# Graph attention on one core: part of the weighted row sums moved to TensorE, h.u as a matmul, q kept in SBUF, and the short last tile transferred in two pieces

## The chip, the core and the metric

The kernel runs on one core of a Trainium2 chip. The core has five engines with queues of their own: TensorE (PE, matrix products; loading of the stationary operand is shown as PEld), VectorE (DVE), ScalarE (ACT), GpSimd (POOL) and SyncE (SP). SP, ACT and POOL issue DMA transfers. SBUF is the on-chip working memory with 128 partitions; PSUM is the accumulator memory that TensorE writes. The metric is the time of one execution in device microseconds (us), lower is better. The kernel before is timed in three runs; a profile comes from one more execution.

## The reference: what is computed

One layer of graph attention over N = 3327 nodes with D = 1024 features, in float32. With h the layer-normed x passed through a ReLU:

```python
f = h @ Wf + bf
g = h @ Wg + bg
e = relu(f @ g.T)
scores = where(adj > 0, e, -9e15)
out = x + softmax(scores, axis=1) @ (h @ W + bW)
```

The adjacency matrix has few ones: a node has at most some 37 neighbours. So for node i only its neighbours j are needed:

- score(i, j) = relu(h_j . q_i + c_i), where q_i = A^T h_i + v with A = Wf Wg^T, v = Wg bf, and c_i = h_i . u + c with u = Wf bg, c = bf . bg;
- y_i = the sum over the neighbours of softmax weight times h_j;
- out_i = x_i + y_i W + bW.

## The kernel before

The program has two stages on the core.

**The first stage** walks over 26 tiles of 128 nodes; the last holds 127, since 3327 = 25 x 128 + 127. For each tile, `degrees` (L428) loads the rows of adj into `a` (L431, on SP's queue), turns them to float with their row sum on ACT (L433) and multiplies by the column number on POOL (L434). `normed` (L400) loads the x rows into `xt` (L404, SP), normalizes them and writes them to the DRAM table `hd` (L426, ACT's queue). `edges` (L439) picks the neighbour lists with MAX8 on DVE (L443 to L454); `store_lists` (L468) writes them to the DRAM table `pd`. Beside that `make_A` (L502) builds the product A on TensorE and ScalarE, 128 rows at a time, and u, which L517 makes as a row repeated in all partitions (`u_sb`). At the end the nodes are sorted by their number of neighbours; L583 writes the permutation `perm`. After it `make_rows` (L520) makes the constants; the last of its copies, on DVE, is L354.

**The second stage** walks over 26 tiles of the sorted nodes. `CAPS` gives the largest number of neighbours in each tile, from 37 down to 11. For a tile s:

- `prepare(s)` (L635) gathers the lists (`pi`) and the rows of h (`hp`) with indirect DMA on POOL, transposes hp on TensorE (`hT`), multiplies by A into `q` in PSUM (L648, L649), and takes c_i = h.u + c on DVE with a multiply-and-sum over 1024 elements (L658, into `ci`).
- `dot(s, k)` (L665) gathers the rows of the k-th neighbour of all 128 nodes into one of 23 buffers `G` (L669, POOL) and multiplies them with q on DVE, adding ci (L671). Each such instruction is followed by a short one that reads the accumulator.
- `softmax` (L676) turns the scores into weights `sc`: maximum on DVE, exp on ACT (L687). A tile with more than 20 neighbours is done in two chunks, and the second rescales y by `al` (L692).
- `combine` (L700) makes y, the weighted sum: the first neighbour on ACT (L709), every further one as one multiply-add on DVE (L711), in a chain over y. For two chunks y is divided by the sum of weights on ACT (L713).
- `project(s)` (L715) gathers the x rows (`xp`), transposes y on TensorE (L619) with copies to SBUF on ACT (L620), and multiplies by W (L726, L727). `finish(s)` (L730) adds x on DVE (L735) and scatters the rows to the output (L736, POOL).

TensorE does a float32 product as two instructions, so eight products show as 16.

The order of the program is the loop at the end: prepare one tile ahead, the dots of a chunk, finish of the tile before, softmax, the first three dots of the next chunk, combine, project. The framework plans from this the order of each engine's instructions, by its own estimate of times, and places the waits; an instruction that is ready can be put ahead of an earlier one that is not. On the chip each engine keeps to the planned order. Buffers are limited: 23 for G, two for hp, y and xp, one for hT; a gather waits until the buffer's last reader is done.

## Time and profile before

| What | Value |
|---|---|
| median of three runs | 1794.35 us (1793.04 to 1795.7) |
| profiled execution, its own time | 1794.12 us |
| its span, first to last instruction | 1792.4 us |
| mean granted TensorE clock | 0.81 |
| busy: DVE, PE, POOL, ACT | 82%, 60%, 46%, 17% of the span |
| q0 (POOL's indirect transfers) | 286.92 MB |
| all transfers | 372.37 MB, mean 208 GB/s |

A line of a group names the source line, the engine, the operation, what it writes and reads, the shapes and the count; then busy us and mean ns of one, and the idle time of the engine just before such instructions with what ended most of it. A line of the timeline names start and length in us, engine, line and operation; in square brackets stand the idle time before it and what released it. A DMA line names the queue's engine, the count, KB each and the median us from issue to landing. Times in windows count from the start of the span.

### The profile page before, as it was taken

How to read it: one execution, taken by the hardware profiler on the slowest of the kernel's cores; microseconds unless marked ns; L12 is line 12 of the kernel's file. 1: busy time of each engine (PE TensorE's matmuls, PEld its weight loads, DVE VectorE, ACT ScalarE, POOL GpSimd, SP SyncE). 2: the span in 40 equal slices, each digit the busy share in tenths (PEclk: the TensorE clock that was granted, in tenths of full speed). 3: DMA queues.
4: the chain of work that ended last, by engine and by line, in shares of the span. 5: the costliest groups of instructions: out<-in, count | busy, mean ns of one | idle time of the engine just before them, and what ended most of it. 6: DMA issues, size and time to landing. Idle time of an engine off the chain costs nothing.

```text
span 1792.4 us, 10947 instructions
## 1 busy us (share of the span) xinstructions
PE 1069.6 (60%) x2824; PEld 493.0 (28%) x2824; DVE 1478.6 (82%) x2798; ACT 296.9 (17%) x480; POOL 827.9 (46%) x625
## 2 busy tenths in 40 slices
PE   1278980354007736477364777766686959697833
PEld 1134440021003313133131333323332424233311
DVE  5877860377999899999999999999999899988850
ACT  6666650100001011011000000000000001000100
POOL 7667570115455344553455544444454445435510
PEclk9999995567558868788687888888898979898866
DMA  8888850029678576773676655655665656646320
GB/s 319 306 329 298 292 190 27 28 84 376 210 233 292 168 223 222 236 238 137 222 270 224 242 214 191 226 197 211 212 244 203 232 191 252 205 170 214 100 65 17
DMA packets 124312, 372.37 MB, mean 208 GB/s; under 512 B 40905, under 2 KB 41305, under 8 KB 120913
## 3 DMA queue, kind: packets, MB, share of 16 engines
q0 software_dynamic: 106288, 286.92, 46.8%
q1 hardware_dynamic: 10800, 70.49, 10.7%
q10 hardware_dynamic: 7152, 14.18, 2.1%
q8 instruction: 24, 0.39, 0.1%
q14 instruction: 48, 0.39, 0.1%
HBM read 343.63 MB, written 27.80 MB: 207 GB/s over the span
## 4 chain that ended last, share of the span: by engine, by line
DVE 27%; PE 27%; issue 22%; POOL 9%; DMA 7%; another core or an unknown queue 4%; ACT 2%; POOLq 0%; ACTq 0%; DVEq 0%
DVE y L711 15%; PE ps_o L726 14%; PE q L648 8%; POOL r L434 5%; DVE junk L671 5%; DMA G<-hd,pi 4%; POOL G L608 3%; DVE cand L443 2%; PE ps_A L511 2%; PE ps_t L619 2%; DMA hd<-xt 1%; ACT r L433 1%; DVE sc L671 1%; DVE lst L450 1%
## 5 line engine op out<-in xcount | busy, mean ns | idle before, releaser
L608 POOL DMA_INDIRECT G<-hd,pi x468 | 505.2, 1080 | 418.8 <-DVE y L711 163.3
L671 DVE CUSTOM_DVE_ANT_0 junk<-G,q,ci 128x1024 bf16<-128x1024 f32 (+1 forms) x468 | 597.3, 1276 | 44.6 <-DMA G<-hd,pi 26.4
L711 DVE SCALAR_TENSOR_TENSOR y<-G,sc,y 128x1024 f32<-128x1024 f32 (+1 forms) x442 | 566.2, 1283 | 32.1 <-ACT y L709 23.0
L726 PE MATMUL ps_o<-W_sb,yT 128*128 128x512 f32 (+1 forms) x832 | 402.6, 640 | 1.3 <-ACT yT L620 1.3
L648 PE MATMUL q<-A_sb,hT 128*128 128x512 f32 (+1 forms) x832 | 372.6, 601 | 14.1 <-ACT hT L620 7.5
L619 PE MATMUL ps_t<-ident,y 128*128 128x128 f32 (+1 forms) x208 | 48.1, 408 | 488.6 <-DVE y L711 267.9
L434 POOL TENSOR_TENSOR r<-r,iotaj 128x3327 f32<-128x3327 f32 (+1 forms) x26 | 188.3, 7250 | 131.8 <-ACT r L433 127.4
L726 PEld LDWEIGHTS ps_o<-W_sb,yT 128*128 128x128 f32 (+1 forms) x832 | 166.9, 207 | 207.0 <-issue 198.1
L648 PEld LDWEIGHTS q<-A_sb,hT 128*128 128x128 f32 (+1 forms) x832 | 154.4, 190 | 201.6 <-issue 187.4
L619 PEld LDWEIGHTS ps_t<-ident,y 128*128 128x128 f32 (+1 forms) x208 | 38.7, 214 | 495.6 <-issue 273.1
L443 DVE MAX8 cand<-r 128x8 f32<-128x208 f32 (+2 forms) x416 | 134.0, 360 | 47.9 <-POOL r L434 47.9
L511 PE MATMUL ps_A<-WgT,WfT 128*128 128x512 f32 x256 | 126.3, 655 | 0.5 <-ACT WfT L483 0.5
L620 ACT COPY yT<-ps_t 128x512 f32<-128x512 f32 (+1 forms) x52 | 29.9, 585 | 521.3 <-PE ps_t L619 521.3
L608 POOL DMA_INDIRECT hp<-hd,perm x26 | 27.8, 1068 | 172.0 <-PE ps_t L619 118.7
L433 ACT ACTIVATE r<-a 128x3327 f32<-128x3327 int32 (+1 forms) x26 | 77.1, 2967 | 56.4 <-DMA a<-in_adj_dram 54.7
L608 POOL DMA_INDIRECT xp<-in_x_dram,perm x26 | 34.6, 1329 | 94.7 <-DMA out_dram<-xp,perm 83.1
L410 DVE BATCH_NORM_STATS2 st<-xt 128x6 f32<-128x512 f32 (+1 forms) x26 | 17.7, 680 | 69.2 <-DMA xt<-in_x_dram 69.2
L511 PEld LDWEIGHTS ps_A<-WgT,WfT 128*128 128x128 f32 x256 | 53.0, 211 | 76.6 <-issue 68.4
L687 ACT ACTIVATE sc<-sc,nm 128x11 f32<-128x11 f32 (+11 forms) x32 | 9.8, 308 | 372.6 <-DVE nm L683 272.6
L620 ACT COPY hT<-ps_t 128x512 f32<-128x512 f32 (+1 forms) x52 | 28.0, 588 | 251.4 <-PE ps_t L619 226.8
L736 POOL DMA_INDIRECT out_dram<-xp,perm x26 | 31.8, 1222 | 74.0 <-DVE rs L696 34.0
L466 PE MATMUL pre<-oh,low 128*128 128x64 bf16 x26 | 5.4, 207 | 101.5 <-DVE hit L463 101.5
(131 smaller groups left out, 746.9 us busy)
## 6 DMA issues: line engine op xcount, KB each, us to landing
a<-in_adj_dram SPq DMA_DIRECT2D x25, 1663.5 KB, 9.4
xt<-in_x_dram SPq DMA_DIRECT2D x25, 512.0 KB, 4.3
hd<-xt ACTq DMA_DIRECT2D x25, 512.0 KB, 6.7
G<-hd,pi POOLq DMA_INDIRECT x468, 5.9
wr<-in_L_gnn_Wg_dram SPq DMA_DIRECT2D x8, 512.0 KB, 6.4
wr<-in_L_gnn_Wf_dram SPq DMA_DIRECT2D x8, 512.0 KB, 6.6
W_sb<-in_L_gnn_W_dram SPq DMA_DIRECT2D x1, 4096.0 KB
a<-in_adj_dram SPq DMA_DIRECT2D x1, 1650.5 KB
```

Of the source, the lines that this page charges most:

```text
L433: nc.scalar.activation(r[:n], a[:n], AF.Relu, accum_out=deg[:n, t : t + 1])
L434: nc.gpsimd.tensor_mul(r[:n], r[:n], iotaj[:n])
L443: nc.vector.max(cand[:n, s * 8 : s * 8 + 8], r[:n, s * SW : min(N, (s + 1) * SW)])
L511: nc.tensor.matmul(ps, WfT[:, k, :], WgT[:, k, o * CB : (o + 1) * CB], start=(k == 0), stop=(k == KD - 1))
L608: nc.gpsimd.indirect_dma_start(out=to, out_offset=None, in_=table, in_offset=bass.IndirectOffsetOnAxis(ap=idx, axis=0),)
L619: nc.tensor.transpose(ps[:, k, :n], of[:n, (g + k) * P : (g + k + 1) * P], ident[:n, :n])
L620: nc.scalar.copy(to[:, g : g + 4, :n], ps[:, :, :n])
L648: nc.tensor.matmul(qo, hT[:, k, :n], A_sb[:, k, o * CB : (o + 1) * CB], start=(k == 0), stop=False)
L671: nc.vector.tensor_tensor_reduce(junk[:n], g[:n], e["q"][:n], 1.0, e["ci"][:n], op0=ALU.mult, op1=ALU.add, accum_out=e["sc"][:n, k : k + 1],)
L711: nc.vector.scalar_tensor_tensor(y, G[s, k][:n], p, y, op0=ALU.mult, op1=ALU.add)
L726: nc.tensor.matmul(ps[:n], yT[:, k, :n], W_sb[:, k, o * CB : (o + 1) * CB], start=(k == 0), stop=False)
L736: ins = nc.gpsimd.indirect_dma_start(out=out[:, :], out_offset=bass.IndirectOffsetOnAxis(ap=perm[:n, s : s + 1], axis=0), in_=e["xp"][:n], ...
```

## The change

Three things are changed.

1. **The short tile's transfers.** A new `pieces(t)` cuts the 127 rows of the last tile into 112 and 15. The loads of x and adj, the store of hd and the store of the lists issue one transfer for each piece. Tiles of 128 rows are one piece as before. The indirect transfers of the second stage are not cut.
2. **h.u and q.** u is made as a column per 128 features (`uT`), and `prepare` multiplies hT by it on TensorE: eight products with one column into a PSUM tile, from which ACT makes ci, adding c. L658 and its DVE instruction are gone. q goes to PSUM in halves, and ACT copies each half to a tile in SBUF (`qpool`, two buffers). The call of prepare moves from the start of tile s (for s + 1) to the end of tile s (for s + 2), after project(s); prepare(0) and prepare(1) stand before the loop. The PSUM room that q leaves takes the new tile `yT_ps`.
3. **A part of the weighted sums on TensorE.** `on_tensor` picks m neighbours of a tile's last chunk, m = (4 cap - 52) / 5 rounded down, at least 0 and at most two less than the chunk has, spread evenly and never k = 0. For each of them ACT makes a diagonal matrix from the weights (`diag`, four buffers), and TensorE multiplies the eight 128-column blocks of G by it, which adds the weighted rows, already transposed, in `yT_ps`. The other neighbours stay on DVE. In project, y is added to the same PSUM tile by eight products with the identity, in place of its eight transposes; where m is 0 the transposes stay. The division by the sum of weights is now made on the weights (sc) and on al, ahead of the rescaling of y, so L713 is gone.

```diff
+    def pieces(t):
+        n = rows(t)
+        m = n - n % 16
+        return [(0, m), (m, n - m)] if 0 < m < n else [(0, n)]
...
-            nc.sync.dma_start(xt[:n], x[t * P : t * P + n, :])
+            for a, m in pieces(t):
+                nc.sync.dma_start(xt[a : a + m], x[t * P + a : t * P + a + m, :])
...
-                nc.tensor.matmul(ps, bgr[:, k, :], WfT[:, k, :], start=(k == 0), stop=(k == KD - 1))
-            nc.scalar.copy(u_sb[:, c * P : (c + 1) * P], ps)
+                nc.tensor.matmul(ps[:, 0:1], WfT[:, k, :], bgT[:, k : k + 1], start=(k == 0), stop=(k == KD - 1))
+            nc.scalar.copy(uT[:, c : c + 1], ps[:, 0:1])
...
-        q = p_q.tile([P, D], FP, name="q")
+        q = e["q"] = qpool.tile([P, D], FP, name="q")
...
+            nc.scalar.copy(q[:n, o * CB : (o + 1) * CB], ps[:n])
+        ps = p_t.tile([P, 4, P], FP, name="ps_t")
+        for k in range(KD):
+            nc.tensor.matmul(ps[:n, 0, 0:1], hT[:, k, :n], uT[:, k : k + 1], start=(k == 0), stop=(k == KD - 1))
+        ci = e["ci"] = small.tile([P, 1], FP, name="ci")
+        nc.scalar.activation(ci[:n], ps[:n, 0, 0:1], AF.Identity, bias=c_sb[:n])
...
-        nc.vector.tensor_tensor_reduce(
-            junk[:n], hp[:n], u_sb[:n], 1.0, c_sb[:n], op0=ALU.mult, op1=ALU.add, accum_out=ci[:n]
-        )
...
+        if last:
+            rs = small.tile([P, 1], FP, name="rs")
+            nc.vector.reciprocal(rs[:n], l[:n])
+            if k0:
+                nc.vector.tensor_tensor(al[:n], al[:n], rs[:n], op=ALU.mult)
+            nc.vector.tensor_scalar(sc, sc, rs[:n], None, op0=ALU.mult)
+        if k0:
             nc.scalar.activation(e["y"][:n], e["y"][:n], AF.Copy, scale=al[:n])
...
+    def on_tensor(s, k0, k1):
+        m = min(max(0, (4 * CAPS[s] - 52) // 5), k1 - k0 - 2)
+        ks = range(max(k0, 1), k1)
+        return [k for i, k in enumerate(ks) if (i + 1) * m // len(ks) > i * m // len(ks)]
...
+            if k in pe:
+                diag = dpool.tile([P, P], FP, name="diag")
+                nc.scalar.activation(diag[:n, :n], ident[:n, :n], AF.Copy, scale=p)
+                if e["yT"] is None:
+                    e["yT"] = p_y.tile([P, KD, P], FP, name="yT_ps")
+                for c in range(KD):
+                    nc.tensor.matmul(
+                        e["yT"][:, c, :n], g[:n, c * P : (c + 1) * P], diag[:n, :n],
+                        start=(k == pe[0] and c % 4 == 0), stop=False, skip_group_check=True,
+                    )
...
+            for c in range(KD):
+                nc.tensor.matmul(
+                    e["yT"][:, c, :n], e["y"][:n, c * P : (c + 1) * P], ident[:n, :n],
+                    start=False, stop=(c % 4 == 3), skip_group_check=True,
+                )
+            for g in range(0, KD, 4):
+                nc.scalar.copy(yT[:, g : g + 4, :n], e["yT"][:, g : g + 4, :n])
...
     prepare(0)
+    prepare(1)
     for i, (s, k0, k1) in enumerate(units):
-        if not k0 and s + 1 < NT:
-            prepare(s + 1)
...
             project(s)
+            if s + 2 < NT:
+                prepare(s + 2)
```

More of the change, by code (lines that the diff above doesn't have):

```diff
@@ L333, in edge_path @@
     A_sb = wts.tile([P, KD, D], FP, name="A_sb")
-    u_sb = wts.tile([P, D], FP, name="u_sb")
+    uT = wts.tile([P, KD], FP, name="uT")
     c_sb = wts.tile([P, 1], FP, name="c_sb")
@@ L425, in normed @@
             nc.scalar.activation(xt[:n], xt[:n], AF.Relu, bias=nmr[:n], scale=rstd[:n])
-            nc.scalar.dma_start(hd[t * P : t * P + n, :], xt[:n])
+            for a, m in pieces(t):
+                nc.scalar.dma_start(hd[t * P + a : t * P + a + m, :], xt[a : a + m])
         def degrees(t):
@@ L430, in degrees @@
             a = apool.tile([P, N], I32, name="a")
-            nc.sync.dma_start(a[:n], adj[t * P : t * P + n, :])
+            for b, m in pieces(t):
+                nc.sync.dma_start(a[b : b + m], adj[t * P + b : t * P + b + m, :])
             r = kpool.tile([P, N], FP, name="r")
@@ L474, in store_lists @@
             if t1 > full:
-                nc.scalar.dma_start(pd[full * P :, :], pay[: rows(full), full, :])
+                for b, m in pieces(full):
+                    nc.scalar.dma_start(pd[full * P + b : full * P + b + m, :], pay[b : b + m, full, :])
         def transposed(to, of):
@@ L604, in edge_path @@
     p_t = ctx.enter_context(tc.tile_pool(name="p_t", bufs=2, space=PSUM))
+    p_y = ctx.enter_context(tc.tile_pool(name="p_y", bufs=1, space=PSUM))
     p_o = ctx.enter_context(tc.tile_pool(name="p_o", bufs=2, space=PSUM))
@@ L620, in transposed2 @@
             nc.scalar.copy(to[:, g : g + 4, :n], ps[:, :, :n])
-    def times(pool, name, lT, w_sb, b3, n):
-        halves = []
-        for o in range(OH):
-            ps = pool.tile([P, CB], FP, name=f"{name}{o if pool is p_q else ''}")
-            for k in range(KD):
-                nc.tensor.matmul(ps[:n], lT[:, k, :n], w_sb[:, k, o * CB : (o + 1) * CB], start=(k == 0), stop=False)
-            nc.tensor.matmul(ps[:n], ones3[:, :n], b3[:, o * CB : (o + 1) * CB], start=False, stop=True)
-            halves.append(ps)
-        return halves
     st = {}
@@ L776, in edge_path @@
     nc.vector.tensor_reduce(bad, bads, AX.X, ALU.max)
-    onesf = small.tile([P, P], FP, name="onesf")
+    onesf = small.tile([P, 1], FP, name="onesf")
     nc.vector.memset(onesf, 1.0)
```

31 lines of the change are left out of this document (14 added, 17 removed).

## The prediction

> **What bounds the kernel now.** I read the busy table by stages first, then the groups of the second half, then the timeline where the table shows a hole. Columns of the stage table: PE, PEld, DVE, ACT, POOL busy us with instruction counts, granted TensorE clock, DMA share, GB/s.
>
> ```profile
> 269.00:339.00 70.00, 0.22 (x1) 0.10 (x1) 0.78 (x2) 5.01 (x7) 8.85 (x2) 0.52 0.06 26
> 590.00:905.00 315.00, 186.87 (x466) 83.57 (x465) 298.47 (x423) 32.69 (x60) 144.42 (x135) 0.79 0.65 210
> 1250.00:1600.00 350.00, 270.41 (x682) 120.49 (x681) 320.17 (x439) 30.66 (x58) 169.48 (x156) 0.88 0.62 220
> 1690.00:1792.00 102.00, 36.65 (x86) 16.75 (x86) 34.42 (x44) 3.88 (x7) 14.67 (x7) 0.68 0.21 54
> ```
>
> There are three things to see. From 269 to 339 us every engine stands still while 26 GB/s trickle in. From 590 to 1600 DVE is busy 91 to 95% of the time: it sets the pace of the tile loop, with PE second. After 1690 nothing is busy; the last tile hangs on transfers of 127 rows, and the change leaves those as they are.
>
> The hole, in order of time, with the DMA issue table:
>
> ```profile
> 246.18 3.35 SPq L431 DMA_DIRECT2D a<-in_adj_dram  x2
> 263.43 7.23 POOL L434 TENSOR_TENSOR r<-r,iotaj 128x3327 f32<-128x3327 f32 x1 [2.76 <-ACT r L433]
> 268.40 14.06 SPq L404 DMA_DIRECT2D xt<-in_x_dram  x1
> 318.58 2.98 ACT L433 ACTIVATE r<-a 127x3327 f32<-127x3327 int32 x1 [54.65 <-DMA a<-in_adj_dram]
> 338.40 0.69 DVE L410 BATCH_NORM_STATS2 st<-xt 127x6 f32<-127x512 f32 x1 [69.22 <-DMA xt<-in_x_dram]
> 347.15 0.33 DVE L443 MAX8 cand<-r 127x8 f32<-127x208 f32 x1
> 352.78 22.23 DMA hd<-xt
> 372.18 0.18 DVE L583 SCALAR_TENSOR_TENSOR perm<-ps_u,tens 128x26 int32<-128x26 f32 x1
> 376.04 1.25 POOL L608 DMA_INDIRECT hp<-hd,perm  x1 [47.12 <-issue]
> 380.73 1.28 DVE L658 CUSTOM_DVE_ANT_0 junk<-hp,u_sb,c_sb 128x1024 bf16<-128x1024 f32 x1 [4.40 <-issue]
> ...
> a<-in_adj_dram SPq DMA_DIRECT2D x25, 1663.5 KB, 9.4
> xt<-in_x_dram SPq DMA_DIRECT2D x25, 512.0 KB, 4.3
> hd<-xt ACTq DMA_DIRECT2D x25, 512.0 KB, 6.7
> ```
>
> A full tile of a lands in 9.4 us; the one of 127 rows, issued by 249.5, lands at 318.6, 69 us later. The x rows behind it land at 338.4, and the write of hd takes 22.2 us instead of 6.7.
>
> **Part 1, the last tile's transfers in two.** Nothing but these transfers holds the stage. I leave the issue of the x rows at 268.4; they land at 268.4 + 4.3 = 272.7 instead of 338.4: 65.7 earlier. From there to the permutation the trace has 372.2 - 338.4 = 33.8 us of work, which gives 306.5. What is late next is POOL: its product for the last tile follows the one that ends at 270.7, ends near 277.9, and the path from the first MAX8 on it to the permutation is 372.2 - 347.2 = 25.0, so 302.9: not later. hd is issued 14.4 us after the x rows and lands at 272.7 + 14.4 + 6.7 = 293.8. So the gather that stood at 376.0 starts at 306.5: **-69.5**. Bounds: were the 15-row pieces as slow as the trace's 127-row ones, a would need 15/127 of 69 us, 8 more, and the rest 2 to 3 each, which still leaves -60; -75 if the waits inside the 33.8 us go too. SP and ACT each issue one or two more transfers, about 0.33 us each, where they otherwise stand. In the Trainium skill, "DMA: Bandwidth & Descriptors", section "Why a DMA increments its semaphore by 16 and not by 1", a transfer runs on the largest number of engines, up to 16, that divides its rows: 127 gives one, 112 sixteen, 15 fifteen; by that the pieces cost next to nothing. The 26 GB/s row agrees for 127; no row here shows 112 or 15.
>
> **Part 2, h.u on TensorE.**
>
> ```profile
> L671 DVE CUSTOM_DVE_ANT_0 junk<-G,q,ci 128x1024 bf16<-128x1024 f32 x458 | 584.5, 1276 | 24.8 <-PE q L649 11.4 <-DMA G<-hd,pi 6.5
> L711 DVE SCALAR_TENSOR_TENSOR y<-G,sc,y 128x1024 f32<-128x1024 f32 x429 | 549.5, 1283 | 30.6 <-ACT y L709 21.8 <-ACT y L692 2.2
> L671 DVE DVE_READ_ACCUMULATOR2_ANT sc<- 128x1 f32 x457 | 37.1, 81 | 0.0
> L735 DVE TENSOR_TENSOR xp<-ps_o,xp 128x512 f32<-128x512 f32 x48 | 33.0, 688 | 13.3 <-PE ps_o L727 13.2
> L658 DVE CUSTOM_DVE_ANT_0 junk<-hp,u_sb,c_sb 128x1024 bf16<-128x1024 f32 (+1 forms) x24 | 30.7, 1278 | 0.1
> L696 DVE RECIPROCAL rs<-l 128x1 f32<-128x1 f32 x25 | 4.0, 162 | 6.3 <-ACT sc L687 6.1
> ```
>
> These are DVE's groups from 416 to 1690 us. L658 goes: 24 x (1.278 + 0.081) = **-32.6**, all on DVE. The first two stand earlier, with a 4.4 us wait for hp ahead of them, in front of the work that lets the lists be gathered: 4.4 + 0.5 + 2 x 1.3 = **-7.5** (0 if q's own chain ends later).
>
> **q in SBUF costs nothing on DVE:** L658 reads both operands from SBUF and takes 1278 ns, the dot with q in PSUM 1276. Two ACT copies a tile of about 0.59 us (below) lie on an engine busy 33 of 315 us. prepare(s+1) followed project(s-1) before and does so now; the order in the program is the same.
>
> **Part 3, a fifth of the sums on TensorE.** The formula gives m = 16 for the first tile, 9, 8, 7, 6, 6, 5, 5, 4, 4, 4, 4, 3, 3, 3, 2, 2, 1, 1, 1 and then 0: 94 of 442 sums in 20 tiles. The price on either engine:
>
> ```profile
> 1195.64 1.28 DVE L671 CUSTOM_DVE_ANT_0 junk<-G,q,ci 128x1024 bf16<-128x1024 f32 x1
> 1196.97 1.28 DVE L671 CUSTOM_DVE_ANT_0 junk<-G,q,ci 128x1024 bf16<-128x1024 f32 x1
> 1198.71 0.31 ACT L687 ACTIVATE sc<-sc,nm 128x17 f32<-128x17 f32 x1 [14.87 <-DVE nm L683]
> 1202.57 13.17 DVE L711 SCALAR_TENSOR_TENSOR y<-G,sc,y 128x1024 f32<-128x1024 f32 x10 [1.76 <-ACT y L709]
> 1217.13 1.28 DVE L711 SCALAR_TENSOR_TENSOR y<-G,sc,y 128x1024 f32<-128x1024 f32 x1
> 1219.53 1.28 DVE L711 SCALAR_TENSOR_TENSOR y<-G,sc,y 128x1024 f32<-128x1024 f32 x1
> 1247.75 0.31 ACT L687 ACTIVATE sc<-sc,nm 128x17 f32<-128x17 f32 x1 [14.62 <-DVE nm L683]
> ...
> 266.26 1.95 PE L517 MATMUL ps_u<-WfT,bgr 128*128 128x128 f32 x16
> 372.47 3.54 PE L524 MATMUL ps_u<-bfT,bgr 128*128 128x1 f32 x16 [0.55 <-PE ps_u L577]
> 674.63 1.10 PE L619 MATMUL ps_t<-ident,hp 128*128 128x128 f32 x8
> 1201.06 7.13 PE L648 MATMUL q<-A_sb,hT 128*128 128x512 f32 x16 [0.29 <-ACT hT L620]
> 1208.12 0.38 PE L649 MATMUL q<-v,ones 3*128 3x512 bf16 x1
> 1230.56 1.94 PE L619 MATMUL ps_t<-ident,y 128*128 128x128 f32 x8 [14.68 <-DVE y L711]
> ```
>
> A sum alone costs 13.17 / 10 = 1.32 us; alternating with dots, two sums start 2.40 apart, and a dot alone needs 1.33, so such a sum is worth 1.08. Bounds 94 x 1.08 = 102 and 94 x 1.32 = 124. In the tile shown six of 16 sums alternate, so I take 1.22: **-115**.
>
> On PE a moved sum is eight f32 products of 128x128, 16 instructions: 1.95 us by L517. The other PE work of a tile: q and out each 2 x (7.13 + 0.38) = 15.0, transposes 1.1, y added by eight products 1.95, the u column 2 to 3.54, waits for copies some 1.2: 36.3. So PE needs 36.3 + 1.95 m. DVE needs 1.32 per dot, 1.32 per remaining sum and about 5 us of rest (two L735, softmax, the 1.76 wait on y); as a check, before the change this gives 22.4 + 21.1 + 5 + 1.3 = 49.8 for 17 neighbours, and the trace has 1247.75 - 1198.71 = 49.0. After it:
>
> 17 neighbours: DVE 44.6, PE 42.1. 20: 49.9 and 46.0. 18: 45.9 and 44.1. 12: 35.4 and 36.3. Over all 26 tiles DVE 1222, PE 1127.
>
> DVE stays the bound, with PE at 92% beside it. The diagonals hide on ACT:
>
> ```profile
> L620 ACT COPY yT<-ps_t 128x512 f32<-128x512 f32 x48 | 27.6, 585 | 486.8 <-PE ps_t L619 486.8
> L518 ACT COPY u_sb<-ps_u 128x128 f32<-128x128 f32 x8 | 2.1, 263 | 4.5 <-PE ps_u L517 3.2 <-PE pre L461 1.2
> ```
>
> 94 x 0.26 = 25 us on ACT (above 0.26, and below the 1.16 that a 1024-wide y takes). If ACT were not free, DVE would wait at the softmax for them.
>
> **What it adds to DVE's path.** Six tiles work in two chunks: reciprocal, al x rs and the scaling of sc now stand before y's rescaling, about 0.7 us each, 4. In the first tile PE takes 16 of 18 sums, 31.2 us, while DVE has two; only 5 of the 23 G buffers are free, so the next eight gathers follow PE's 1.95 instead of 1.32, plus one landing (4.3 to 6.7 by the issue table): 5 + 6. With a late q behind it: **+18** (5 to 30). Then waits between two nearly full engines: DVE already waits 11.4 for q and 13.2 for ps_o, and ci now comes after q, from PE through ACT. As much again in doubled work on PE, less what its steadier clock gives back: **+18** (0 to 50).
>
> **The sum**, against the profiled execution's 1794.12 (span 1792.4; the median of the runs is 1794.35): -69.5 - 7.5 - 32.6 - 115 + 18 + 18 = -188.6, so **1606**.
>
> **A rule against the change, weighed.** The rows first:
>
> ```profile
> 1206.29 1.01 POOL L608 DMA_INDIRECT G<-hd,pi  x1 [0.30 <-issue]
> 1625.38 0.94 POOL L608 DMA_INDIRECT G<-hd,pi  x1 [0.30 <-issue]
> ```
>
> A gather issued beside sums (two SBUF operands) takes 1.01, beside dots (q in PSUM) 0.94. With q in SBUF all would take 1.01 plus the gap of 0.30, just under DVE's 1.32: no cost. The Trainium skill, "SBUF — State Buffer", section "Who interferes with whom", says that DVE instructions with two SBUF inputs contend with GpSimd ones that read SBUF, and that the later one blocks entirely. By that every gather would wait out a dot; the rows beside sums do not show it.
>
> **The rivals.**
>
> *PE becomes the bound.* After a wait PE runs slowly: the eight products on y take 1.94 (1230.56), the same eight on hp 1.10 (674.63). If the new products start cold, a moved sum costs 1.95 x 1.77 = 3.45 and the u column 3.54; a tile needs 37.8 + 3.45 m, which is above DVE for every tile of 16 neighbours or more, by 86 us in all. Less the 18 already counted: 1672. Against it: PE is now rarely idle.
>
> *PE holds G buffers.* Freed late, they block POOL's queue, in which gathers stand in order. With 20 neighbours only three buffers are spare; a diagonal 7 us late delays the dots. At 5 us in the nine tiles of 17 to 20: 1650.
>
> *POOL is blocked by dots on SBUF.* Each gather 0.94 + 1.28 + 0.30 = 2.5 us, 468 of them 1179, against a loop of 1274 - 33 - 115 + 36 = 1162; bunched as they are by the buffers coming free, about 1640.
>
> *The split does nothing*, the 112 rows still going at 26 GB/s: 1606 + 69 = 1675.
>
> *Slower: exp queues behind PE on ACT.* ACT's instructions run one after another as they stand, and now q's copies and ci, which end PE's chain for the next tile, share it with exp. Today exp waits only for DVE (1198.71). Were ci of the next tile put before exp, DVE would wait until PE has done out, hT, q and u, about 36 us after the last combine, where its 17 dots take 24: 12 us a tile, 8 to 15 by size, 25 x 11 = 275, so 1880. It decides from 188.6 / 25 = 7.5 us a tile on. Against it: the order today follows readiness, and L696 waits only 6.1 us in all.
>
> **How the numbers follow.** Forecast 1606 with its own range 1568 to 1640: 0.62. PE bound 0.14, buffers 0.08, no split 0.06, blocked POOL 0.03, exp behind PE 0.04, more gain than all bounds 0.03. The range 1565 to 1690 covers the forecast and the rivals below 1680. 0.2%, about 3.6 us, is what a measurement can tell from no change; only exp in some tiles lands there: same 0.01, slower 0.04, faster 0.95.
>
> **What would show it.** Right: no hole near 269 to 339 and the first hp gather near 306; L658's group gone; the remaining sums 348 at 1.28; dots still near 1.28; DVE 90% or more busy in the loop, with PE near 85 to 90% and a higher clock. Wrong: 16 products on a diagonal well above 2 us, DVE waiting at the dots for ci or G, the reciprocal waiting on exp by microseconds, or a transfer of 112 rows at 26 GB/s.

## The result, and the profile after

The changed kernel takes **1548.44 us** (median of four runs, 1547.99 to 1551.25) beside 1793.98 for the kernel before: a ratio of 0.8634, with a 95% interval of 0.8619 to 0.8649. The forecast was 1606, the range 1565 to 1690; the result lies 17 us below the range. The profiled execution took 1548.85, with a span of 1547.1 and a granted TensorE clock of 0.92 (0.81 before).

First the end of the first stage in the changed kernel, from its timeline, and from its table of DMA issues between 200 and 292 us the sizes of the pieces:

```profile
259.67 0.88 SPq L411 DMA_DIRECT2D xt<-in_x_dram  x2
291.54 0.18 DVE L593 SCALAR_TENSOR_TENSOR perm<-ps_u,tens 128x26 int32<-128x26 f32 x1
292.01 1.08 POOL L621 DMA_INDIRECT hp<-hd,perm  x1 [20.46 <-DVE perm L593]
328.53 1.28 DVE L673 CUSTOM_DVE_ANT_0 junk<-G,q,ci 128x1024 bf16<-128x1024 f32 x1 [5.87 <-DMA G<-hd,pi]
1481.86 0.30 ACT L689 ACTIVATE sc<-sc,nm 127x11 f32<-127x11 f32 x1 [25.84 <-DVE nm L685]
...
a<-in_adj_dram SPq DMA_DIRECT2D x1, 1455.6 KB, 10.4
xt<-in_x_dram SPq DMA_DIRECT2D x1, 448.0 KB, 3.8
xt<-in_x_dram SPq DMA_DIRECT2D x1, 60.0 KB, 3.6
```

The hole is gone: 112 rows of a land in 10.4 us, 15 rows of x in 3.6, where 127 rows of a had taken 69. The first gather of hp starts at 292.0 instead of 376.0.

The first dot (328.53) and the last tile's exp (1481.86) cut the span in three. In the kernel before they stood here:

```profile
416.27 1.28 DVE L671 CUSTOM_DVE_ANT_0 junk<-G,q,ci 128x1024 bf16<-128x1024 f32 x1 [5.61 <-DMA G<-hd,pi]
1728.01 0.30 ACT L687 ACTIVATE sc<-sc,nm 127x11 f32<-127x11 f32 x1 [28.35 <-DVE nm L683]
```

So the **start** gave 87.7 us, the **loop** between them went from 1311.7 to 1153.3, 158.4 less, and the **tail** stayed at 65.

The loop by stages (columns as in the prediction's first table), and DVE's two large groups and TensorE's new one between 420 and 1480 us:

```profile
420.00:900.00 480.00, 474.41 (x2169) 295.66 (x2168) 449.75 (x677) 79.53 (x184) 298.36 (x254) 0.98 0.77 266
900.00:1240.00 340.00, 332.34 (x1209) 179.72 (x1207) 321.72 (x473) 48.14 (x107) 225.62 (x174) 0.96 0.77 257
1240.00:1480.00 240.00, 188.43 (x526) 89.98 (x525) 188.83 (x252) 24.37 (x47) 120.14 (x82) 0.87 0.57 175
...
L673 DVE CUSTOM_DVE_ANT_0 junk<-G,q,ci 128x1024 bf16<-128x1024 f32 (+1 forms) x423 | 542.5, 1282 | 29.4 <-DMA G<-hd,pi 19.0 <-ACT ci L657 7.9
L734 DVE SCALAR_TENSOR_TENSOR y<-G,sc,y 128x1024 f32<-128x1024 f32 x318 | 408.7, 1285 | 12.2 <-ACT y L732 8.1 <-ACT y L701 2.4
L727 PE MATMUL yT_ps<-diag,G 128*128 128x128 f32 x1404 | 164.7, 279 | 0.9 <-ACT diag L723 0.9
```

From 420 to 900 us the two engines are nearly full together: PE is busy 99% and DVE 94%. A moved sum costs PE 164.7 / (1404 / 16) = 1.88 us. DVE waits little at its dots, 7.9 us for ci and 19 for G.

What the groups don't show is the order of PE's work. From PE's timeline between 870 and 950 us, the rows that show it:

```profile
889.84 7.03 PE L650 MATMUL ps_q<-A_sb,hT 128*128 128x512 f32 x16
904.50 0.66 PE L632 MATMUL ps_t<-ident,hp 128*128 128x128 f32 x4
905.00 1.93 PE L655 MATMUL ps_t<-uT,hT 128*128 128x1 f32 x16
908.80 3.78 PE L746 MATMUL yT_ps<-ident,y 128*128 128x128 f32 x16 [1.23 <-DVE y L734]
913.32 9.14 PE L756 MATMUL ps_o<-W_sb,yT 128*128 128x512 f32 x16 [0.73 <-ACT yT L751]
```

PE makes the q (889.84) and the u column (905.00) of a tile to come, and transposes of hp, *before* it takes up the present tile's y (908.80), and waits 1.2 us for y. In the kernel before it waited 14.7 us for y (1230.56 in the prediction's rows), and only then made out, and the next hT and q. That is a different order, and the prediction had said that the order stays.

### The profile page after: what moved, and what is told of

It is laid out like the page before. It is cut to its first block, busy times and chain, and to the rows that moved or that the text cites. A ratio compares the mean times of both kernels' runs of the same rounds, so it can differ in the third digit from the quotient of the medians.

```text
span 1547.1 us, 15226 instructions
## 1 busy us (share of the span) xinstructions
PE 1282.8 (83%) x4904; PEld 718.8 (46%) x4904; DVE 1314.7 (85%) x2664; ACT 350.9 (23%) x646; POOL 920.8 (60%) x625
## 4 chain that ended last, share of the span: by engine, by line
PE 50%; issue 12%; DVE 8%; POOL 5%; DMA 3%; ACT 1%; POOLq 0%; ACTq 0%; DVEq 0%
PE ps_o L756 19%; PE ps_q L650 15%; PE yT_ps L727 8%; DVE y L734 5%; POOL G L621 4%; PE yT_ps L746 2%; PE ps_t L655 2%; DVE junk L673 2%; DMA G<-hd,pi 2%; PE ps_t L632 1%; PE ps_o L757 1%; PE ps_q L651 1%; DMA xp<-in_x_dram,perm 1%; DVE xp L765 0%; ACT hT L633 0%
## 5 line engine op out<-in xcount | busy, mean ns | idle before, releaser
L621 POOL DMA_INDIRECT G<-hd,pi x468 | 599.2, 1280 | 313.9 <-DVE y L734 128.1
L734 DVE SCALAR_TENSOR_TENSOR y<-G,sc,y 128x1024 f32<-128x1024 f32 (+1 forms) x348 | 447.2, 1285 | 14.6 <-ACT y L732 9.4
L650 PE MATMUL ps_q<-A_sb,hT 128*128 128x512 f32 (+1 forms) x832 | 384.1, 612 | 29.3 <-ACT q L652 24.2
L650 PEld LDWEIGHTS ps_q<-A_sb,hT 128*128 128x128 f32 (+1 forms) x832 | 156.2, 195 | 210.5 <-issue 177.7
L727 PE MATMUL yT_ps<-diag,G 128*128 128x128 f32 x1504 | 176.0, 279 | 1.4 <-ACT diag L723 1.4
L727 PEld LDWEIGHTS yT_ps<-diag,G 128*128 128x128 f32 x1504 | 172.9, 195 | 7.0 <-ACT diag L723 3.6
L652 ACT COPY q<-ps_q 128x512 f32<-128x512 f32 (+1 forms) x52 | 29.4, 591 | 295.4 <-PE ps_q L651 203.9
L765 DVE TENSOR_TENSOR xp<-ps_o,xp 128x512 f32<-128x512 f32 (+1 forms) x52 | 35.7, 687 | 43.6 <-PE ps_o L757 43.6
L766 POOL DMA_INDIRECT out_dram<-xp,perm x26 | 37.8, 1452 | 57.3 <-DVE flag L812 28.2
L621 POOL DMA_INDIRECT xp<-in_x_dram,perm x26 | 29.6, 1137 | 69.3 <-DMA out_dram<-xp,perm 64.1
L746 PE MATMUL yT_ps<-ident,y 128*128 128x128 f32 x320 | 48.4, 315 | 20.1 <-DVE y L734 20.1
L746 PEld LDWEIGHTS yT_ps<-ident,y 128*128 128x128 f32 x320 | 46.1, 228 | 23.5 <-DVE y L734 21.8
## 6 DMA issues: line engine op xcount, KB each, us to landing
W_sb<-in_L_gnn_W_dram SPq DMA_DIRECT2D x1, 4096.0 KB, 14.7
a<-in_adj_dram SPq DMA_DIRECT2D x1, 1455.6 KB, 10.4
```

The costliest lines, as they stand in the source:

```text
L621: nc.gpsimd.indirect_dma_start(out=to, out_offset=None, in_=table, in_offset=bass.IndirectOffsetOnAxis(ap=idx, axis=0),)
L650: nc.tensor.matmul(ps[:n], hT[:, k, :n], A_sb[:, k, o * CB : (o + 1) * CB], start=(k == 0), stop=False)
L727: nc.tensor.matmul(e["yT"][:, c, :n], g[:n, c * P : (c + 1) * P], diag[:n, :n], start=(k == pe[0] and c % 4 == 0), stop=False, skip_group_ ...
L734: nc.vector.scalar_tensor_tensor(y, g[:n], p, y, op0=ALU.mult, op1=ALU.add)
L746: nc.tensor.matmul(e["yT"][:, c, :n], e["y"][:n, c * P : (c + 1) * P], ident[:n, :n], start=False, stop=(c % 4 == 3), skip_group_check=True,)
L766: ins = nc.gpsimd.indirect_dma_start(out=out[:, :], out_offset=bass.IndirectOffsetOnAxis(ap=perm[:n, s : s + 1], axis=0), in_=e["xp"][:n], ...
```

## Experiments

**Theories.** D, the forecast's: DVE's own instructions set the pace of the loop, so each instruction taken off it is worth its duration. P: the old loop is a ring through PE as well (y, out, hT, q, first dot, sums, y), closed because y's and hp's transposes share one pair of PSUM buffers, `ps_t`; the change opens it, since with sums on TensorE y's result has a buffer of its own, `yT_ps`. M: the ring is right, but it is the moved sums themselves that shorten it.

The table has all kernels but e8_pitch, whose time says nothing; times in us. The three parts of the span are as above; idle is DVE's, from the end of one instruction to the start of the next, in the loop; a dot is taken with the accumulator read behind it and the 0.04 us that follow that read even where nothing is waited for. The last column counts sums that a dot follows directly. The parts are those of the profiled execution, one of the runs behind the median; in e17_all that was the fastest, 1471.3.

| kernel | median | first dot | loop | tail | DVE idle | sum, then dot |
|---|---|---|---|---|---|---|
| before | 1794 | 416.3 | 1311.7 | 64.4 | 96 | 196 |
| e1_split | 1723.4 | 344.7 | 1312.9 | 64.4 | 98 | 196 |
| e5_hu | 1757.9 | 330.4 | 1360.5 | 65.4 | 171 | 196 |
| e14_u_first | 1719.9 | 329.6 | 1323.3 | 64.4 | 137 | 199 |
| e2_no_sums | 1746.7 | 329.3 | 1350.4 | 64.5 | 158 | 187 |
| e9_own_yT | 1634.8 | 328.9 | 1234.4 | 67.3 | 94 | 322 |
| e10_yT_in_pt | 1665.8 | 329.1 | 1269.1 | 65.4 | 181 | 136 |
| e3_half_sums | 1607.7 | 329.4 | 1217.9 | 64.3 | 107 | 269 |
| **after** | 1548.4 | 328.5 | 1153.3 | 65.3 | 104 | 255 |
| e4_more_sums | 1628.5 | 330.0 | 1225.4 | 66.3 | 213 | 85 |
| e6_in_order | 1651.5 | 329.0 | 1255.1 | 63.3 | 158 | 31 |
| e7_tail | 1564.1 | 328.5 | 1186.3 | 47.9 | 136 | 255 |
| e11_own_all | 1540.9 | 329.5 | 1141.1 | 68.2 | 105 | 281 |
| e12_one_each | 1536.2 | 328.5 | 1134.4 | 71.4 | 102 | 281 |
| e15_one_u_first | 1527.2 | 329.1 | 1127.5 | 69.3 | 93 | 279 |
| e16_one_tail | 1477.1 | 327.9 | 1096.9 | 52.2 | 63 | 281 |
| e17_all | 1476.5 | 329.7 | 1084.5 | 55.3 | 50 | 279 |

The kernel before gave medians of 1793.6 to 1795.8 beside these runs.

### The parts one after another

The split alone, on the kernel before:

```diff
-            nc.sync.dma_start(xt[:n], x[t * P : t * P + n, :])
+            for a, m in pieces(t):
+                nc.sync.dma_start(xt[a : a + m], x[t * P + a : t * P + a + m, :])
   (the same for a, hd and pd)
```

> The kernel before with the last tile's transfers in two pieces and nothing else. By the prediction's step (issue of the x rows left at 268.4 us, 33.8 us of work behind them): first hp gather at 306.5 instead of 376.0, so 1794 - 69.5 = 1724.5. By what the trace of the changed kernel shows (x rows issued at 259.7, the work of tile 24 no longer behind them): the first hp gather near 294, so 1794 - 82 = 1712. If the split were worth nothing by itself: 1794.

1723.41, ratio 0.9601 (0.9584 to 0.9617): 72.3 us less. The first dot comes 71.6 us sooner, and the loop is 1 us longer. The first gather of hp stands at 303.7, the forecast had 306.5. The prediction's step holds, and the guess from the changed kernel's trace, 1712, was the worse one.

On top of it, h.u on TensorE, with q left in PSUM and all sums on DVE:

```diff
-        nc.vector.tensor_tensor_reduce(
-            junk[:n], hp[:n], u_sb[:n], 1.0, c_sb[:n], op0=ALU.mult, op1=ALU.add, accum_out=ci[:n]
-        )
+        ps = p_t.tile([P, 4, P], FP, name="ps_t")
+        for k in range(KD):
+            nc.tensor.matmul(ps[:n, 0, 0:1], hT[:, k, :n], uT[:, k : k + 1], start=(k == 0), stop=(k == KD - 1))
+        nc.scalar.activation(ci[:n], ps[:n, 0, 0:1], AF.Identity, bias=c_sb[:n])
```

> The split and h.u on TensorE; q stays in PSUM, all sums stay on DVE. By the prediction's step, 24 x 1.36 us off DVE and 7.5 us at the start: 40 below the split alone, about 1672 if that gives 1712. If q ends as late as ci did at the start, or ci is now waited for at each tile's first dot: 0 to 25 below it, 1687 to 1712.

1757.92, ratio 0.9797 (0.9777 to 0.9817): 34.5 us **slower** than the split alone, outside everything expected. 14.2 us were won ahead of the first dot and 47.6 lost in the loop. One turn of the ring in this kernel's timeline, and its waits between 420 and 1480 us:

```profile
913.16 1.94 PE L629 MATMUL ps_t<-ident,y 128*128 128x128 f32 x8 [24.27 <-DVE y L721]
914.98 8.98 PE L736 MATMUL ps_o<-W_sb,yT 128*128 128x512 f32 x16
931.58 1.09 PE L629 MATMUL ps_t<-ident,hp 128*128 128x128 f32 x8
932.97 7.13 PE L658 MATMUL q<-A_sb,hT 128*128 128x512 f32 x16 [0.29 <-ACT hT L630]
947.74 1.95 PE L668 MATMUL ps_t<-uT,hT 128*128 128x1 f32 x16
952.52 0.26 ACT L670 ACTIVATE ci<-ps_t,c_sb 128x1 f32<-128x1 f32 x1 [19.12 <-remote]
952.82 1.28 DVE L681 CUSTOM_DVE_ANT_0 junk<-G,q,ci 128x1024 bf16<-128x1024 f32 x1 [4.71 <-DMA G<-hd,pi]
965.04 1.94 PE L629 MATMUL ps_t<-ident,y 128*128 128x128 f32 x8 [15.36 <-DVE y L721]
...
DVE junk L681 <- ACT ci L670: 39.3, 10, 5.2
DVE junk L681 <- issue: 16.3, 5, 4.7
DVE junk L681 <- DMA G<-hd,pi: 14.1, 6, 4.7
```

From y's transposes to the next dot 39.7 us pass: out, hT, q, u, ci one behind another. The split alone has no u column in this ring; there q was done 33.8 us after y's transposes began (914.28 to 948.1 in its trace). The column shows as 1.95 us, but ci starts 4.8 us after the column does (2.0 to 5.1 in the tiles of this loop). DVE's instructions stand in a fixed order, so it stops at the dot with sums still to do. (The third wait in the list has G's name. The dot shown has it too, but starts 0.04 us after ci ends, so it waited for ci.)

Is it ci's place at the end of q's chain, or the third `ps_t` buffer that it takes? The column and ci ahead of q's products:

> As e5_hu (split, h.u on TensorE, q in PSUM, all sums on DVE; 1757.9 us), but the u column and ci are made before q's products instead of behind them. If h.u alone lost because ci ends q's chain 5 us later than q did (DVE waited 39 us for ci and 30 for what then came late), the chain now grows by the column's 2 us only: 1690 to 1710, below the split alone (1723.4). If it lost by the third ps_t buffer that it takes for each tile: 1750 to 1760.

1719.86: 38 us faster than with ci at the end, so the place is what hurt and not the buffer. But only 3.5 us, and not 13 to 33, faster than the split alone: DVE now waits 33.7 us for q, which the column delays in turn. In this order the loop has lost 24 instructions of 1.28 us on DVE, 30.8 us, and is 10 us longer than the split's; DVE's idle time has grown by 39. D is wrong for the old loop.

q in SBUF, prepare two tiles ahead in the program, and everything else of the change, but no sums on TensorE:

```diff
     def on_tensor(s, k0, k1):
-        m = min(max(0, (4 * CAPS[s] - 52) // 5), k1 - k0 - 2)
+        m = 0
```

> The changed kernel with all 442 sums on DVE and ACT again (none on TensorE); split, h.u and q in SBUF stay. By the prediction's price of 1.22 us a sum and its surcharges of 36 us for the sums' waits: 1548.4 + 115 - 36 = 1627. If those surcharges were never there, 94 sums at 1.21 to 1.31: 1662 to 1671. If PE's work on the sums had been a bound in places: below 1627.

1746.68, ratio 0.9726 (0.9705 to 0.9747), above everything expected: the 94 sums are worth 198 us in the changed kernel, 2.1 us each, and no sum on DVE takes that long (1.20 to 1.32). Half of them:

> The changed kernel with 42 instead of 94 sums on TensorE (half of each tile's number, rounded down). If each moved sum is worth the same (no price for waits): 1548.4 + 52 x 1.21 to 1.31 = 1611 to 1617. If the second half of the sums pays for waits between two nearly full engines, its worth is smaller: 1570 to 1600, and the first half is worth more.

1607.74: the first 42 sums bring 139 us (3.3 each), the other 52 bring 59 (1.14 each). The first ones do something besides being moved.

### What they do: the PSUM buffer

With m = 0, y goes through `transposed2`, that is through `ps_t`, as before. The next two kernels separate the buffer from the sums. First no sums on TensorE, but y's transposes into `yT_ps`:

```diff
         if e["yT"] is None:
-            transposed2(yT, e["y"], n)
+            ps = p_y.tile([P, KD, P], FP, name="yT_ps")
+            for c in range(KD):
+                nc.tensor.transpose(ps[:, c, :n], e["y"][:n, c * P : (c + 1) * P], ident[:n, :n])
+            for g in range(0, KD, 4):
+                nc.scalar.copy(yT[:, g : g + 4, :n], ps[:, g : g + 4, :n])
```

> No sums on TensorE, as in e2_no_sums (1746.7 us), but the transposes of y go to a PSUM buffer of their own (yT_ps) instead of the pair of ps_t buffers that hT and the u column use too; PE's order then has q's chain ahead of y's transposes. Theory P (in the kernel without sums on TensorE DVE waits for ci, because the shared ps_t pair holds hT behind y, and the sums on TensorE removed that only because their result has its own PSUM): the 60 to 72 us of waits go, 1675 to 1690, and the 94 sums then have a worth of 1.3 to 1.5 us each. Theory M (the moved sums themselves shorten the chain from y to ci): no change, 1740 to 1750.

**1634.80**, ratio 0.9112 (0.9090 to 0.9134): 112 us below e2_no_sums for a PSUM buffer of y's own, more than theory P had dared. Then the reverse, all 94 sums on TensorE but accumulated in the pair of `ps_t`:

```diff
-                    e["yT"] = p_y.tile([P, KD, P], FP, name="yT_ps")
+                    e["yT"] = [p_t.tile([P, 4, P], FP, name="ps_t") for _ in range(2)]
```

> The changed kernel with all its 94 sums on TensorE, but accumulated in the pair of ps_t buffers that hT and the u column use too, instead of yT_ps. Theory P: PE's order has out, hT, q and u after y again, DVE waits for ci at the first dot by 3 to 5 us in some 20 tiles: 1600 to 1650. Theory M: 1545 to 1555.

1665.83, ratio 0.9301 (0.9261 to 0.9340): 117 us lost, a little more than P had expected. M is out. The four kernels make a square:

| | y through the shared ps_t | y in yT_ps | the buffer is worth |
|---|---|---|---|
| no sums on TensorE | 1746.7 | 1634.8 | 112 |
| 94 sums on TensorE | 1665.8 | 1548.4 | 117 |
| the sums are worth | 81 | 86 | |

The two parts add up almost cleanly, and the sums by themselves bring 0.86 to 0.92 us each. One rival is left: yT_ps also adds room, as much again as the pair has. No run gave the shared pool more buffers instead, so whether it is the sharing or the number of buffers that closes the ring isn't told apart. Two turns in the timelines show the mechanism, first without sums and with the shared pair (e2_no_sums), then with the buffer (e9_own_yT):

```profile
908.35 1.94 PE L632 MATMUL ps_t<-ident,y 128*128 128x128 f32 x8 [28.23 <-DVE y L734]
910.16 8.61 PE L756 MATMUL ps_o<-W_sb,yT 128*128 128x512 f32 x16
926.40 1.09 PE L632 MATMUL ps_t<-ident,hp 128*128 128x128 f32 x8
948.56 1.34 DVE L673 CUSTOM_DVE_ANT_0 junk<-G,q,ci 128x1024 bf16<-128x1024 f32 x1 [4.76 <-ACT ci L657]
```

```profile
909.89 7.13 PE L650 MATMUL ps_q<-A_sb,hT 128*128 128x512 f32 x16
925.15 1.93 PE L655 MATMUL ps_t<-uT,hT 128*128 128x1 f32 x16
938.40 1.97 PE L745 MATMUL yT_ps<-ident,y 128*128 128x128 f32 x8 [10.82 <-DVE y L734]
941.89 7.03 PE L760 MATMUL ps_o<-W_sb,yT 128*128 128x512 f32 x16
...
DVE junk L673 <- DMA G<-hd,pi: 34.6, 18, 16.8
DVE xp L769 <- PE ps_o L761: 12.5, 17, 2.9
```

With the shared pair PE stands 28.2 us for y, and the next tile's q comes after out. With the own buffer q and the column run while DVE still sums; DVE's waits for ci (28.7 us in e2_no_sums) pass out of its list, and those for the lists shrink from 11.5 to 1.1 us. By the table that is 64 us of idle time. The other 52 us of the loop's 116 are DVE's instructions following each other more closely (dots 25 us less, sums 17, the small ones 10): with q there early, dots stand between the sums, 322 times instead of 187, and such a pair is done faster (below).

The Trainium skill, "Perfetto Trace Analysis", section "Matmuls", asks that independent matmul groups rotate through different PSUM banks so that the evacuation of one overlaps the products of the next. The square shows a case close to it, with a price, 112 to 117 us: the section speaks of banks and of evacuation, and what held PE here was two uses that take turns in one pair of buffers.

### How much more TensorE can take

Up to three sums more in each tile, 159 in all:

```diff
-        m = min(max(0, (4 * CAPS[s] - 52) // 5), k1 - k0 - 2)
+        m = min(max(0, (4 * CAPS[s] - 52) // 5 + 3), k1 - k0 - 2)
```

> The changed kernel with up to three more sums a tile on TensorE, 159 instead of 94. If DVE is still the only bound: 1548.4 - 65 x 1.1 = 1477. If PE is the bound by now (it is busy 99% from 420 to 900 us): 65 more at 1.83 us, 119, less the some 60 us in which PE is idle after 900 us: 1600 to 1625. If both are equally near: 1540 to 1570.

1628.48, 80 us slower, just above what PE as the bound gives. Its stages:

```profile
420.00:900.00 480.00, 458.77 (x2329) 301.46 (x2329) 416.95 (x631) 83.71 (x197) 279.23 (x244) 0.98 0.74 256
900.00:1240.00 340.00, 336.54 (x1505) 205.22 (x1504) 265.41 (x376) 51.21 (x115) 177.63 (x160) 0.99 0.67 237
1240.00:1480.00 240.00, 238.22 (x932) 135.51 (x931) 193.45 (x276) 35.55 (x78) 117.68 (x101) 0.98 0.60 205
```

PE is busy 96 to 99% throughout, DVE 78 to 87%. But the planned order also changed (q right behind out again in the tiles between 860 and 960 us, 62 us of waits for ci), so PE's load and that order aren't told apart.

### Sums and dots in turn

DVE's dots and sums held in the program's order:

```diff
-        nc.vector.tensor_tensor_reduce(
+        in_order(nc.vector.tensor_tensor_reduce(
   (and the sums likewise; in_order adds an edge of order, without a wait, from the dot or sum traced before)
```

> The changed kernel with DVE's dots and sums held in the order of the program: three dots of the next chunk ahead of the sums, then all sums, then the other dots, so that they no longer alternate. The 255 places where a dot follows a sum at 1.21 us then cost 1.285 (sum after sum) and 1.33 (dot after dot): 255 x (0.075 + 0.12) = 50, 1598, if DVE sets the pace and waits no more than before. If PE sets it (99% busy from 420 to 900 us), 1550 to 1570. If sums run through also free G buffers later and start gathers late: above 1620.

1651.47, 103 us slower. The dots and sums themselves took 43 us more (dots from 582 to 608 us, sums from 414 to 431, by start to start), close to the 50 expected; idle time grew by 54. That is above 1620, as the third expectation had it, but by two waits for ci (35 us) and by those for out (34 us instead of 26), not for gathers.

The pitches by themselves, in six blocks of 24 instructions behind the last tile, in one run:

> The changed kernel with six blocks of 24 DVE instructions of 1024 elements behind its last tile, held in order, each with eight gathers on POOL beside it; its time is the changed kernel's plus some 210 us and says nothing. Start to start: sums chained over one y 1.28 to 1.29, sums over two y's in turn 1.21 if it is the dependence on y that costs, else 1.28; dots with q in SBUF 1.33, with q in PSUM 1.33; dot and sum in turn 1.21 each, with q in PSUM as well as in SBUF. Gathers beside dots on SBUF 1.0 or 1.7 if they wait out a part of a dot; beside dots on PSUM 0.94.

Instructions of one kind without a gap show as one row. Chained sums, sums over two y's in turn, then a dot after a dot on q in SBUF, then a sum after a dot:

```profile
1533.11 30.34 DVE L820 SCALAR_TENSOR_TENSOR y<-G,sc,y 128x1024 f32<-128x1024 f32 x23
1564.72 27.86 DVE L820 SCALAR_TENSOR_TENSOR y<-G,sc,y 128x1024 f32<-128x1024 f32 x23
1619.20 1.28 DVE L823 CUSTOM_DVE_ANT_0 junk<-G,q,sc 128x1024 bf16<-128x1024 f32 x1
1620.53 1.28 DVE L823 CUSTOM_DVE_ANT_0 junk<-G,q,sc 128x1024 bf16<-128x1024 f32 x1
1673.39 1.28 DVE L820 SCALAR_TENSOR_TENSOR y<-G,sc,y 128x1024 f32<-128x1024 f32 x1
1674.59 1.27 DVE L823 CUSTOM_DVE_ANT_0 junk<-G,q,sc 128x1024 bf16<-128x1024 f32 x1
1675.80 1.27 DVE L820 SCALAR_TENSOR_TENSOR y<-G,sc,y 128x1024 f32<-128x1024 f32 x1
```

Chained sums start every 1.32 us (1.28 to 1.29 was expected), sums on two y's every 1.20 (1.23 to 1.25 while the gathers run): the dependence on y costs 0.12. Dots start every 1.33 with q in SBUF and every 1.325 with q in PSUM; in turn each costs 1.20. So a dot put between two sums saves 0.12 + 0.13 us, and q's place saves nothing.

### The last tiles

Six tiles have no sums on TensorE and so still use `ps_t`. With `yT_ps` for them too, by the edit of e9_own_yT on the changed kernel:

> The changed kernel, and the last six tiles, which have no sums on TensorE and so still transpose y through the shared ps_t pair, use yT_ps too. Theory P: in the six tiles DVE is busy 79% of 1240 to 1480 us where the kernel with its own buffer in all tiles and no sums on TensorE has 91% there: 20 to 30 us of waits go, 1518 to 1530. Theory M, or the last tiles held by their transfers: 1543 to 1553.

1540.93, 7.5 us less (one of the four runs took 1550.5): the sign of P, a third of its size. With at least one sum moved in every tile, which gives them the buffer as well:

```diff
-        m = min(max(0, (4 * CAPS[s] - 52) // 5), k1 - k0 - 2)
+        m = min(max(1, (4 * CAPS[s] - 52) // 5), k1 - k0 - 2)
```

> The changed kernel with at least one sum on TensorE in every tile, so that the last six tiles have yT_ps by the product itself; six more sums move. Theory P: as with the buffer alone, less 6 x 1.2: 1510 to 1525. Theory M: six sums at 1.1 us, 1540 to 1545.

1536.19, ratio 0.8566 (0.8544 to 0.8587), between the two expectations. A part of what is left hangs on the tile of 127 rows in the second stage, which the change left alone. The edit for it, with `permz` a copy of the last 15 indices that starts at partition 0:

```diff
     def prepare(s):
-        n = rows(s)
+        n = P
   ...
-        ins = nc.gpsimd.indirect_dma_start(out=out[:, :], ... ap=perm[:n, s : s + 1] ..., in_=e["xp"][:n], ...)
+        for a, m in pieces(s):
+            to = permz[:m, :] if a else perm[:m, s : s + 1]
+            ins = nc.gpsimd.indirect_dma_start(out=out[:, :], ... ap=to ..., in_=e["xp"][a : a + m], ...)
```

On the changed kernel itself:

> The changed kernel with the last sorted tile worked on as 128 rows (the 128th a copy of node 0 that isn't stored) and its scatter in 112 and 15 rows. If the 127-row gathers and the scatter hold the end as they held the first stage: the gathers of the last tile come without the 9 us of waits, the scatter lands some 14 us sooner: 1548.4 - 20 to 30 = 1518 to 1528. If the end hangs on the chain of y, out and the add alone: 1545 to 1550.

1564.11, 15.7 us slower: the tail gave 17.4 us, near what was expected, and the loop took 33 (waits for out 42 us instead of 26, for exp 21 instead of 5). Does the edit itself cost that? The same edit on e12_one_each, whose expectation puts the loss down to an order made anew:

> As e12_one_each (1536.2 us) with the last sorted tile as 128 rows and its scatter in two. The tail from the last exp on was 17.4 us shorter in e7_tail, and its loop 33 us longer. If that loss came from an order of the instructions made anew and not from the transfers: 1536 - 17 = 1519, within 10 of it. If the 128-row transfers themselves hold up the loop: 1545 to 1555.

**1477.13**, ratio 0.8220 (0.8201 to 0.8238): 59 us less than without it, 19 in the tail and 37 in the loop. So the 128-row transfers don't hold up the loop; those of 127 rows had been holding it, and by far more than expected. Up to 1290 us the traces of e12_one_each and e16_one_tail stay within 3 us of each other; the 37 us come behind that, at dots that wait for G.

The loss in e7_tail stays open, and it is not an order made anew. By the tiles that they write and read, PE, DVE, ACT and POOL run through the same sequence of instructions in e7_tail as in the changed kernel, but for the second piece of the scatter; the same holds for e16_one_tail and e12_one_each. The traces of the first pair part early, long before the last tile. ACT's copy of the second half of a q, first in the changed kernel, where its products end at 340.3 us, then in e7_tail, where they end at 340.2:

```profile
340.36 0.59 ACT L652 COPY q<-ps_q 128x512 f32<-128x512 f32 x1 [6.79 <-PE ps_q L651]
354.85 0.59 ACT L656 COPY q<-ps_q 128x512 f32<-128x512 f32 x1 [21.40 <-remote]
```

By the exps e7_tail is 10 us behind at 463 us, 38 at 824 and 45 at 1115; at the last one it is 33. Why that copy starts 14.5 us late isn't known.

In e12_one_each a stretch behind the last tile's gather of hp (issued at 1264.7 us, 2.65 us long; columns as in the prediction's first table), one of that tile's gathers of G and the longest wait for one, and DVE's waits for G between 420 and 1480 us; then those waits in e16_one_tail:

```profile
1286.00:1300.00 14.00, 10.57 (x25) 4.10 (x23) 7.10 (x10) 0.58 (x1) 0.00 (x0) 1.00 0.06 25
1435.14 2.53 POOL L621 DMA_INDIRECT G<-hd,pi  x1 [0.30 <-issue]
1449.98 1.29 DVE L673 CUSTOM_DVE_ANT_0 junk<-G,q,ci 127x1024 bf16<-127x1024 f32 x1 [15.76 <-DMA G<-hd,pi]
...
DVE junk L673 <- DMA G<-hd,pi: 55.8, 24, 15.8
```

```profile
DVE junk L678 <- DMA G<-hd,pi: 10.2, 8, 2.4
```

A gather of 127 rows holds POOL for 2.5 us where one of 128 takes 0.94, and its rows come late: 15.8 us of wait at one dot. From 1286 to 1300 us a DMA share of 0.06, one sixteenth, moves 25 GB/s, as it did in the first stage's hole (0.06 and 26). The Trainium skill, "DMA: Bandwidth & Descriptors", section "Why a DMA increments its semaphore by 16 and not by 1", puts 127 rows on one engine and 128 on sixteen, with an exception for some direct copies that GpSimd issues. The share of 0.06 fits one engine of sixteen for this gather too.

The column ahead of q in e12_one_each, and all three edits together:

> As e12_one_each (1536.2 us) with the u column and ci ahead of q's products. If ci at the end of the chain still costs something there (DVE waited 7.9 us for it in the changed kernel): 1525 to 1532. If PE's own load is all that counts there: 1533 to 1540.

> The edits of e12_one_each, e15_one_u_first and e16_one_tail in one kernel. If they add up: 1505 to 1515. If each makes the order of instructions anew and the gains are lost in that: 1525 to 1550.

1527.23 and 1476.51 (ratio 0.8227, 0.8211 to 0.8244). The column's place brings 9 us beside e12_one_each and nothing beside the tail's edit. DVE's waits in e12_one_each have none for ci; what shrinks is its wait for the lists, from 9.3 to 1.9 us. Both expectations for e17_all lie above its time, since e16_one_tail alone was already below them. e16_one_tail and e17_all are the fastest of the study and can't be told from each other; both are 4.6% below the changed kernel.

## Why the prediction was wrong

By medians, the parts as the runs separate them and as the forecast had them:

| part | forecast | measured | from |
|---|---|---|---|
| split transfers | -69.5 | -72.3 | before to e1_split |
| h.u on TensorE | -40.1 | +34.5 | to e5_hu |
| q in SBUF, prepare moved | 0 | -11.2 | to e2_no_sums |
| y's own PSUM buffer | not seen | -111.9 | to e9_own_yT |
| 94 sums on TensorE | -79 | -86.4 | to after |
| sum | -188.6 | -247.3 | |

The forecast's -79 is its -115 with both surcharges of 18.

**Right: the split.** The step, its start point 268.4 and the 33.8 us behind it gave 306.5; alone it gave 303.7. In the changed kernel the gather stands 11.7 us earlier still, and in e5_hu, where u is made as a column as well, it stands at 293.1; which instruction there gave way isn't shown.

**Right in sign, too large: the first two L658.** 7.5 was forecast. From the permutation to the gather of pi the kernel with the split alone takes 27.1 us, the changed one 22.6: 4.5.

**The step that failed: "prepare(s+1) followed project(s-1) before and does so now; the order in the program is the same".** The program's order was the same and PE's was not. What the order of PE hung on was a buffer: y's transposes and hp's took turns in two `ps_t`, so hT could not be made before yT was copied. The prediction didn't speak of `p_y`. The change adds that pool in one line and takes q out of PSUM; the buffer, 112 us, is worth more than any other part of the loop.

**With it failed "L658 goes: = -32.6, all on DVE".** DVE busy 91 to 95% was read as DVE setting the pace. In the ring of the old order DVE's share only fills the time until the next q: 30.8 us of work less in e14_u_first came back as 39 us more of idle time. Work taken off DVE there doesn't shorten the ring, and ci at the end of q's chain lengthens it (+34.5 instead of -40.1). The prediction did name ci behind q as a wait and priced it within the second +18.

The two errors have opposite signs: +75 for h.u, -112 for the buffer, and the smaller -11, -7 and -3 make the 58 us between forecast and result. The parts are in the order in which the runs added them; another order would share them out otherwise, as the +34.5 of h.u, measured in the old ring, shows. The -11 is q in SBUF with prepare two tiles ahead, and which of the two brings it wasn't separated.

**Right in size, and in part by luck: the sums.** 1.22 less the waits, 0.84 net, was forecast; 0.86 to 0.92 was measured. Neither surcharge was measured by itself, and the second also covered ci, which belongs to h.u. PE, forecast at 92%, is 99% busy up to 900 us.

**The signs of being right didn't separate the theories.** The hole is gone, dots and sums still take 1.28 us, DVE is 94% busy up to 900 us and the clock rose, all as the prediction named them, and its account of the loop is wrong all the same.

**The rivals.** "PE becomes the bound" didn't come about as priced, 1672, since eight diagonal products take 1.88 us and not 3.45; the granted clock over the span is 0.92. PE may well be the next bound: 65 more sums cost 80 us, though the order changed with them. "PE holds G buffers" stayed small, 19 us of waits for G. "Exp queues behind PE" didn't occur (5.4 us of waits behind exp), but its mechanism, a tile's first dot that waits for PE's chain through ci, is what e5_hu shows. "POOL blocked by dots on SBUF" didn't decide (see the section on the hardware). What came, "more gain than all bounds", had been given 0.03.

## What to carry to other kernels

Ask of every tile pool that a change adds, splits or empties what its buffers had been ordering: two uses that take turns in one PSUM pair are a dependence that no data shows, and here it was worth 112 us. An engine that is busy 93% doesn't have to set the pace; look for the ring of waits that returns to the same instruction one tile later, and shorten that ring; work taken off elsewhere gives nothing back. A part of a change that looks like pure gain can be a loss by itself and right beside another part, so price parts in the order of the engine that runs them, and check what one partition short of 128 costs wherever a tile is transferred.

## What was new about the hardware

- The pitch of 1024-wide f32 instructions on DVE depends on the neighbour: 1.32 us for a sum that needs the last one's y, 1.20 for one that doesn't; 1.33 for a dot after a dot, 1.20 after a sum. In turn both start closer together than their own recorded duration of 1.28.
- q in PSUM or in SBUF makes 0.004 us of difference to a dot. Gathers beside dots with two SBUF operands took 1.02 us, beside dots on PSUM 0.94; beside independent sums the gathers took 0.94 and the sums were recorded at up to 1.33 instead of 1.27. In the changed kernel 103 of 468 gathers took about 1.7 us, each after a pause of POOL; before it were 11, while 131 others behind a pause took some 1.0. The Trainium skill, "SBUF — State Buffer", section "Who interferes with whom", says that two SBUF inputs on DVE contend with a GpSimd instruction that reads SBUF, and calls the lock exclusive. Its sentence that the other side blocks for the whole instruction is on DVE's 2-port modes. For dots the runs show at most some 1.1 us more on POOL (2.0 instead of 0.94, gathers of 128 rows) and 0.07 more on DVE, never a full dot of 1.28.
- A column product (16 instructions of 128x1) is recorded at 1.95 us. In the loop of e5_hu its reader on ACT starts 2.0 to 5.1 us after its start. In the turn shown nothing stands between them; in some tiles it stands right behind the recorded end. What the longer ones wait for isn't shown, so the reader's start is the figure to use.
- A gather of 127 rows costs POOL 2.5 us to issue, and one of 128 rows 0.94.
